# Mixing into z instead of the probabilities' buffer, and moving three weights' sums in a two-layer graph attention kernel

## The chip, the cores and the metric

The kernel runs on one core of a Trainium2 chip. Its time is the device time of one execution in microseconds (us); the median of three runs before the change is 2912.55 us (2912.05 to 2916.1). The engines are TensorE (PE, with its weight loads listed as PEld), VectorE (DVE), ScalarE (ACT) and GpSimd (POOL); SyncE (SP) issues all the DMA transfers.

## The reference

The input is `x`, 128 graphs of 64 nodes with 768 features, and a boolean adjacency for each graph. Two layers follow, each ended by a residual sum and a layer norm. All of it is float32.

```python
# layer 0: 12 heads of 64
h = einsum('bnd,ade->bane', x, W);  th = tanh(h)
attn = th @ w_src + swap(th @ w_dst)
attn = leaky_relu(attn, 0.2);  attn = where(~adj, -999, attn)
out = elu(softmax(attn) @ h + b)
gate = sigmoid(x @ H_w.T + H_b)
x = layernorm(x + gate * out + (1 - gate) * x)
# layer 1: 6 heads of 128
q, k, v = x @ Wq + bq, x @ Wk + bk, x @ Wv + bv
probs = softmax(q k^T / sqrt(128) + (0 or -9e15 by adj))
x = layernorm(x + (probs @ v) @ Wf + bf)
```

## The kernel before

**Tiles and stages.** Two graphs of 64 nodes make a tile of 128 rows, and two tiles make a pair; there are 64 tiles and 32 pairs. `phase_a` runs layer 0 on one pair after the other and also computes layer 1's values `v`, which it writes to DRAM together with the normalised rows and their transposes. `phase_b` then runs the rest of layer 1 on 16 groups of two pairs. Phase A takes the first 1511 us, phase B the other 1400.

**Products from fewer multiplications.** In phase A each product (h with `W`, the gate with `H_w`, v with `Wv`) is cut into two by two by two blocks and done in seven block products rather than eight (class `Product`). This needs sums of the activations' blocks (`token_sums`, four a pair, on POOL, L258 to L261) and sums of the weights' blocks, which are made once (`weight_sums`, L173). A product has seven steps `i = 0..6` of matmuls (L209); each is followed by an eviction from PSUM: a copy into a `snap` buffer or into the result on ACT (L418, L439, L458), or the sum of the bank and a `snap` on DVE (L441, L460). Step 4 adds onto the bank that the `snap` of step 2 reads, and step 6 onto the bank that DVE reads after step 4, so these matmuls wait for those reads. Phase B's products use another scheme of the same kind with 15 steps (class `Stream`, L875), 11 sums of activations (`group_sum`, L845) and 14 sums of 128x512 for each weight (`weight15_sum`, L167).

**What a tile passes through** (class `Tile0`): `tanh`; `dst_mul` and `src_mul` on POOL (L482, L490) with sums on DVE; a round trip through DRAM that spreads the `dst` part over the rows (`dst_out` L500, `dst_in` L508); `add` on ACT (twelve L532); `mask` and `top` on DVE (L539, L543); `exp` on ACT (twelve L548); `scale` on POOL (L558); `probs`, six transposes on PE (L569) and two copies on ACT into the buffer `pt` (L574); `aggregate`, the matmuls with `pt` as one operand (L587); `elu`, which adds the bias into `z` on DVE (L608) and takes the exponential of `z` on ACT (L616) into a tile `e`; `mix1` and `mix2`, four operations on DVE (L620, L621, L629, L630) that write `e`, and at last the row `xt`; `norm1` (L284, L293, L295 on DVE, then L296, L300, L301 on POOL) and `norm2` (L305 on ACT; in the last pair L639 on DVE); and the store `spill`.

The buffers named `pt`, `z`, `th` and `tmp` exist once each. The tile `e` takes the name `pt`, so it lies where the probabilities were; only the last pair puts it into `th` or `tmp`.

**The order.** It is written out by hand. `at(step, f)` notes a function for a step, and `run` calls all functions step by step; each engine executes its own instructions in this order. Pair `p` begins at step `O[p]`, which is 0, 14, 28 for the first three pairs and then 21 apart: `h` takes steps `o` to `o+6`, the gate `o+7` to `o+13`, and seven steps for the values of an earlier pair fill the rest. The pair's tile 1 has its times counted from `s = o`, tile 0 from `s = o+5` (in the last pair `o+3`): `probs` at `s+24`, `aggregate` at `s+25`, `elu`, `mix1` and `mix2` at `s+26` to `s+28`, the norm after that. So tile 1's `mix2` stands at `o+28` and tile 0's `probs` at `o+29`. After the last pair's gate come three earlier pairs' values, up to `o+34`; the last pair's own values stand at `o+45` to `o+51`, behind its norm, two transposes of its rows and its token sums. Phase B begins right behind them, on DVE with the sums L845.

**Weights.** Wv's four blocks are loaded at steps 10, 15, 20 and 25 (L177) and their twelve sums made on POOL at steps 30 to 52; the first values are due at step 56. Wq and Wk are loaded while the last pair runs; Wq's 14 sums stand on POOL from `o+21`, Wk's on DVE from `o+36`. Wf's sums follow on POOL in phase B.

Of the kernel before, what the change touches and what calls it, by code (L numbers as in the profile page):

```python
# [9 lines left out]
F32 = mybir.dt.float32  # L10
U8 = mybir.dt.uint8
AF = mybir.ActivationFunctionType
ALU = mybir.AluOpType
AX = mybir.AxisListType

P = 128
# [45 lines left out]
def kernel(  # L62
# [31 lines left out]
    nc = tc.nc  # L94
    NB, S, D = x.shape
# [7 lines left out]
    NP = NT // 2  # L103
# [40 lines left out]
    def weight_tile(tag):  # L144
        return wts.tile([P, 7, CH, HALF], F32, name=f"w{tag}", tag=f"w{tag}")
# [19 lines left out]
    def weight15_sum(wb, k, eng):  # L165
        to, a, b, sign = WEIGHT_SUMS[k]
        eng.tensor_tensor(wb[:, to], wb[:, a], wb[:, b], SIGN[sign])  # L167

    def weight_sums(part, eng, ks=range(4)):

        for k in ks:
            to, a, b = ((3, 6, 4), (4, 4, 0), (2, 6, 4), (5, 1, 2))[k]
            eng.tensor_tensor(part(to), part(a), part(b), ALU.subtract)  # L173

    def weight_plain(wb, src, blocks):
        for kh, oh in blocks:
                nc.sync.dma_start(  # L177
                    wb[:, SLOT[kh, oh]],
                    src[kh * HALF : (kh + 1) * HALF, oh * HALF : (oh + 1) * HALF].rearrange(
                        "(p c) o -> p c o", p=P  # L180
                    ),
                )
# [125 lines left out]
    def phase_a(ctx):  # L308
        k6 = ctx.enter_context(tc.tile_pool(name="k6", bufs=2))
        k3 = ctx.enter_context(tc.tile_pool(name="k3", bufs=1))  # L310
# [17 lines left out]
        def load_adj(p):  # L328
            t = small.tile([P, 2, S], U8, name="adj")
            nc.sync.dma_start(t, adj_p[p])  # L330
            st[p]["adj"] = t

        def load(p):
            st[p]["x"] = []
            for i in range(2):
                t = xb[:, (0, 1, 5, 6)[(2 * p + i) % 4]]
                nc.sync.dma_start(t, x_t[2 * p + i])
                st[p]["x"].append(t)
# [40 lines left out]
        w2 = weight_tile(2)  # L379
# [89 lines left out]
        class Tile0:  # L469
# [133 lines left out]
            def elu(self):  # L603

                self.z = k3.tile([P, D], F32, name="z")
                zv = self.z.rearrange("p (j h e) -> p j h e", h=2, e=E)
                for h2 in range(2):
                    nc.vector.tensor_tensor(  # L608
                        zv[:, :, h2, :],
                        self.pos[h2],  # L610
                        b_bc[:, None, :].to_broadcast([P, A // 2, E]),
                        ALU.add,
                    )

                self.e = k3.tile([P, D], F32, name=("th", "tmp")[self.i] if self.last else "pt")
                nc.scalar.activation(self.e, self.z, AF.Exp, bias=neg_one)  # L616

            def mix1(self):
                e, z = self.e, self.z
                nc.vector.scalar_tensor_tensor(e, e, 1.0, z, op0=ALU.min, op1=ALU.max)  # L620
                nc.vector.scalar_tensor_tensor(  # L621
                    e, e, 1.0, self.d["x"][self.i], op0=ALU.subtract, op1=ALU.subtract
                )

            def mix2(self):


                e, xt = self.e, self.d["x"][self.i]
                nc.vector.scalar_tensor_tensor(e, self.g, 1.0, e, op0=ALU.add, op1=ALU.mult)  # L629
                nc.vector.scalar_tensor_tensor(xt, xt, 4.0, e, op0=ALU.mult, op1=ALU.add)  # L630

            def norm1(self):
                self.stats = layernorm(small, self.d["x"][self.i], 4.0 * EPS, self.last)
# [17 lines left out]
        def at(step, *fs):  # L651
            events.setdefault(max(step, 0), []).extend(fs)
# [5 lines left out]
        for c in range(CH):  # L658
            at(0, lambda c=c: weight_sums(lambda s: w0_v[:, s, :, c, :], nc.vector))
            for k in range(4):  # L660
                at(
                    30 + 8 * c + 2 * k,
                    lambda c=c, k=k: weight_sums(lambda s: w2[:, s, c], nc.gpsimd, [k]),
                )
        for oc in range(NC):
            at(oc // 2 + 2, lambda oc=oc: hw_blocks(oc))

        for k, block in enumerate(((0, 0), (1, 0), (0, 1), (1, 1))):
            at(10 + 5 * k, lambda block=block: weight_plain(w2, Wv, [block]))

        at(9, lambda: nc.vector.tensor_scalar_add(b_bc, b_bc, 1.0))

# [3 lines left out]
        for p in range(NP):  # L676
            d, o = st[p], O[p]
            d["p"] = p
            if p:
                at(max(o - 20, 1), lambda p=p: load_adj(p))  # L680
                at(o + 8, lambda p=p: load(p))

            def xb_in(d, i):
                d.setdefault("xp", []).append(blocks(x_t[2 * d["p"] + i]))

            def xT(d, i):
                d.setdefault("T", []).append(turn(d["xp"][i]))

            if p:
                at(max(o - 20, 1), lambda d=d: xb_in(d, 0))  # L690
                at(max(o - 16, 1), lambda d=d: xb_in(d, 1))
                at(o - 6, lambda d=d: xT(d, 0))
                at(o - 5, lambda d=d: xT(d, 1))
                at(o - 4, lambda d=d: sums(d))
            else:
                at(0, lambda d=d: d.update(T=[transposed(t) for t in d["x"]]))
                at(0, lambda d=d: sums(d))
            at(o, lambda d=d: start_h(d))
            at(o + 7, lambda d=d: start_g(d))
            for i in range(7):  # L700
                at(o + i, lambda d=d, i=i: dense(d, "W", i))
                at(o + 7 + i, lambda d=d, i=i: dense(d, "G", i))
            for i, s in ((1, o), (0, o + (3 if p == NP - 1 else 5))):
                t = Tile0(p, i)
                at(s + 6 + (i == 0), t.tanh, t.cap)
                at(s + 7, t.dst_mul)
                at(s + 8, t.src_mul)
                at(s + 9, t.dst_sum, t.dst_out)
                at(s + 10, t.src_sum)
                at(s + 13, t.dst_in)  # L710
                at(s + 16, t.exchange)

                at(s + (15 if i else 17), lambda t=t: t.add(0))
                at(s + (16 if i else 17), lambda t=t: t.add(1))
                at(o + (14 if i else 16), t.gate_in)
                at(o + (17 if i else 18), t.gate)
                n = s - (i == 1)
                at(n + 18, t.mask, t.top)
                at(n + 19, lambda t=t: t.exp(0))
                at(n + 20, lambda t=t: t.exp(1))  # L720
                at(s + 21, lambda t=t: t.scale(0), lambda t=t: t.scale(1))
                at(s + 24, t.probs)
                at(s + 25, t.aggregate)
                at(s + 26, t.elu)
                at(s + 27, t.mix1)
                at(s + 28, t.mix2)
                at(s + 29, t.norm1)
                at(s + 30, t.norm2)
                at(s + 31, t.spill)

            def x1_in(d, i):
                d["xp", i] = blocks(x1_d[2 * d["p"] + i])

            def x1T(d, i, t):
                d["x1T", i] = t
                nc.sync.dma_start(xT_d[d["p"]][:, i], t)

            def x1_sums(d):
                d["T"] = [d["x1T", i] for i in range(2)]
                sums(d)  # L740

            if p < NP - 3:
                v = O[p + 3] + 14
                times = ((1, v - 19, v - 13), (0, v - 16, v - 10))
            elif p < NP - 1:

                v = O[-1] + (21 if p == NP - 3 else 28)
                times = ((1, v - 16, v - 7), (0, v - 15, v - 6)) if p == NP - 3 else (
                    (1, v - 12, v - 7), (0, v - 10, v - 6)
                )  # L750
            if p < NP - 1:
                for i, t0, t1 in times:
                    at(t0, lambda d=d, i=i: x1_in(d, i))
                    at(t1, lambda d=d, i=i: x1T(d, i, turn(d["xp", i])))
                at(times[1][2] + 1, lambda d=d: x1_sums(d))
            else:
                v = o + 45
                for i in range(2):
                    at(o + 43 - i, lambda d=d, i=i: x1T(d, i, transposed(d["x"][i])))
                at(o + 44, lambda d=d: x1_sums(d))  # L760
            at(v, lambda d=d: start_v(d))
            for i in range(7):
                at(v + i, lambda d=d, i=i: dense(d, "V", i))
# [5 lines left out]
        o = O[-1]  # L769
        early = []  # L770
# [7 lines left out]
            at(o + (7 + k if k < 4 else 8 + 2 * k), lambda k=k: load_early(0, Wq, k))  # L778
            at(o + 20 + 2 * k, lambda k=k: load_early(1, Wk, k))
        for k in range(len(WEIGHT_SUMS)):  # L780
            at(o + 21 + k // 2, lambda k=k: weight15_sum(early[0], k, nc.gpsimd))
            at(o + 36 + k, lambda k=k: weight15_sum(early[1], k, nc.vector))
        at(o + 30, lambda: load_T4(0))
        run(events, O[-1] + 80)
        return early
# [402 lines left out]
    with tc.manual_schedule():  # L1188
        with ExitStack() as c:
            early = phase_a(c)  # L1190
# [33 lines left out]
```

## Time and profile before

| stretch of the trace, us | length | PE busy | DVE busy | ACT busy | POOL busy |
|---|---|---|---|---|---|
| 0 to 60 | 60 | 47.18 | 28.07 | 18.22 | 19.83 |
| 60 to 100 | 40 | 37.00 | 30.17 | 29.37 | 25.96 |
| 100 to 140 | 40 | 32.28 | 32.05 | 25.44 | 35.07 |
| 140 to 190 | 50 | 42.31 | 39.99 | 30.34 | 30.36 |
| 240 to 1380 | 1140 | 1112.67 | 825.83 | 697.86 | 612.74 |
| 1430 to 1480 | 50 | 46.37 | 32.05 | 26.52 | 36.60 |
| 1480 to 1511 | 31 | 27.11 | 26.80 | 5.68 | 13.17 |
| 1540 to 2911 | 1371 | 1360.91 | 749.99 | 303.95 | 666.83 |

The profiled execution spans 2910.7 us at a mean granted PE clock of 0.996. The table gives, for stretches of the trace, the microseconds in which each engine was busy. A wait that costs something is one that leaves PE idle; idle time of the others costs nothing by itself.

How to read a line of the profile: `L574 ACT COPY pt<-pa` is line 574 of the kernel, on ACT, a copy from a PSUM tile `pa` into `pt`. In a list of waits, `PE pa L587 <- ACT pt L574: 35.5, 31, 3.0` says that PE's instruction of line 587 sat waiting for ACT's of line 574, 35.5 us in total, 31 times, 3.0 us the longest. A row of the timeline has the start, the duration (from the first to the end of the last, where several are merged), engine, line, operation, tiles, count, and in brackets how long the engine had been idle and for whom.

### The profile page before, as it was taken

Reading aid. Unit: us, or ns where it says so; the run is one execution under the profiler, and the core shown is the slowest. Engines: PE = TensorE matmul, PEld = TensorE weight load, DVE = VectorE, ACT = ScalarE, POOL = GpSimd, SP = SyncE. Lnnn points to the kernel's source line nnn. Section 1 sums busy time; section 2 is a strip of 40 time slices with the busy share of each in tenths; the row PEclk is TensorE's granted clock in tenths of the full one; section 3 lists DMA queues with packets and bytes.
Section 4 is the critical chain, followed back from the end, with each engine's and each line's share of the span. In section 5 each row is a group of like instructions: output and inputs, shape, how many; then the busy total and the mean of one; then the engine's idle time right before and its main releaser. Section 6 shows DMA issues by size and latency. Waiting matters only on the chain.

```text
span 2910.7 us, 50738 instructions
## 1 busy us (share of the span) xinstructions
PE 2831.1 (97%) x18108; PEld 2067.9 (71%) x18108; DVE 1852.5 (64%) x3716; ACT 1206.6 (41%) x3737; POOL 1510.3 (52%) x1633
## 2 busy tenths in 40 slices
PE   8889999999999999999999999999999999999998
PEld 5455555555555555555568888888888888888887
DVE  4886777767777777677765555555555555555556
ACT  4656566565665656656532212222211222211223
POOL 3855555555455554555553454455454455454455
PEclk9999999999999999999999999999999999999999
DMA  6435344353443534435461212122212222212222
GB/s 168 111 110 149 114 138 138 119 153 113 139 135 116 153 117 140 137 110 152 146 212 30 71 61 77 62 81 88 74 59 77 78 67 88 83 56 71 88 82 72
DMA packets 358683, 308.40 MB, mean 106 GB/s; under 512 B 226592, under 2 KB 304160, under 8 KB 358432
## 3 DMA queue, kind: packets, MB, share of 16 engines
q1 hardware_dynamic: 358432, 305.16, 34.4%
q8 instruction: 144, 2.36, 0.3%
q14 instruction: 107, 0.88, 0.1%
HBM read 191.41 MB, written 101.06 MB: 100 GB/s over the span
## 4 chain that ended last, share of the span: by engine, by line
PE 82%; DVE 11%; ACT 3%; issue 1%; POOL 1%; SPq 1%; DMA 1%; DVEq 0%; POOLq 0%; ACTq 0%
PE X L875 42%; PE X L209 33%; DVE pt L629 3%; PE pa L587 2%; PE pb L1015 2%; PE pb L940 2%; DVE pt L620 2%; DVE xb L630 1%; DVE pt L621 1%; ACT pt L616 1%; DVE z L608 1%; PE pb L995 1%; ACT s L548 1%; PE pa L569 1%; ACT pt L574 0%
## 5 line engine op out<-in xcount | busy, mean ns | idle before, releaser
L209 PE MATMUL X<-w,S 128*128 128x384 f32 x2304 | 801.7, 493 | 19.6 <-ACT snap L418 10.3
L875 PE MATMUL X<-S,w 128*128 128x256 f32 x2816 | 664.7, 382 | 1.1 <-DVE S L845 0.8
L209 PEld LDWEIGHTS X<-w,S 128*128 128x128 f32 x2304 | 431.7, 191 | 310.4 <-ACT snap L418 12.5
L209 PE MATMUL X<-w,T 128*128 128x384 f32 x1728 | 599.5, 490 | 5.6 <-ACT snap L418 3.5
L875 PEld LDWEIGHTS X<-S,w 128*128 128x128 f32 x2816 | 525.0, 190 | 73.6 <-DVE S L845 1.5
L209 PEld LDWEIGHTS X<-w,T 128*128 128x128 f32 x1728 | 327.8, 192 | 230.3 <-issue 7.8
L857 POOL TENSOR_TENSOR Sc<-cT 128x256 f32<-128x256 f32 x224 | 161.2, 726 | 405.5 <-PE X L875 399.3
L875 PE MATMUL X<-w,Sc 128*128 128x256 f32 x1408 | 322.5, 381 | 0.8 <-DVE xs L918 0.8
L918 DVE TENSOR_TENSOR xs<-xs,X 128x256 f32<-128x256 f32 x512 | 210.4, 419 | 169.0 <-PE X L875 160.1
L875 PEld LDWEIGHTS X<-w,Sc 128*128 128x128 f32 x1408 | 265.5, 190 | 38.3 <-DVE xs L918 1.6
L548 ACT ACTIVATE s<-s,nmx 128x64 f32<-128x64 f32 x768 | 256.2, 335 | 43.1 <-DVE nmx L543 43.1
L901 DVE TENSOR_TENSOR k<-k,X 128x256 f32<-128x256 f32 x320 | 133.5, 421 | 216.2 <-PE X L875 165.8
L901 DVE TENSOR_TENSOR q<-q,X 128x256 f32<-128x256 f32 x320 | 133.2, 420 | 182.1 <-PE X L875 146.4
L875 PE MATMUL X<-xb,w 128*128 128x256 f32 x960 | 236.6, 379 | 0.0
L305 ACT ACTIVATE xs<-xs,shift,rstd 128x768 f32<-128x768 f32 x62 | 63.5, 1025 | 417.3 <-POOL shift L301 396.8
L896 ACT ACTIVATE k<-X,bk_c 128x256 f32<-128x256 f32 x192 | 91.0, 474 | 305.1 <-PE X L875 305.1
L896 ACT ACTIVATE q<-X,bq_c 128x256 f32<-128x256 f32 x192 | 90.8, 473 | 279.5 <-PE X L875 279.5
L418 ACT COPY snap<-X 128x384 f32<-128x384 f32 x288 | 136.5, 474 | 168.6 <-PE X L209 163.8
L875 PEld LDWEIGHTS X<-xb,w 128*128 128x128 f32 x960 | 181.2, 190 | 24.0
L532 ACT ACTIVATE s<-s,src 128x64 f32<-128x64 f32 x768 | 193.3, 336 | 8.8 <-DMA s<-dst_d 8.6
L482 POOL TENSOR_TENSOR tmp<-th,wd_bc 128x768 f32<-128x768 f32 x64 | 120.9, 1889 | 145.1 <-ACT th L478 145.1
L296 POOL TENSOR_TENSOR rstd<-rstd,neg_half 128x1 f32<-128x1 f32 x126 | 69.1, 548 | 235.7 <-DVE rstd L295 235.4
(129 smaller groups left out, 4085.6 us busy)
## 6 DMA issues: line engine op xcount, KB each, us to landing
xb<-in_x_dram SPq DMA_DIRECT2D x64, 384.0 KB
s<-dst_d SPq DMA_DIRECT2D x128, 192.0 KB
x_d<-xb SPq DMA_DIRECT2D x64, 384.0 KB
xT_d<-T SPq DMA_DIRECT2D x64, 384.0 KB
v_d<-v SPq DMA_DIRECT2D x128, 192.0 KB
xb<-xT_d SPq DMA_DIRECT2D x32, 768.0 KB
xb<-v_d SPq DMA_DIRECT2D x256, 96.0 KB
xs<-x_d SPq DMA_DIRECT2D x64, 384.0 KB
```

The costliest lines, as they stand in the source:

```text
L209: nc.tensor.matmul(o, self.lhsT(i, c), rhs, start=first and c == 0, stop=last and c == CH - 1, skip_group_check=True,)
L296: nc.gpsimd.tensor_tensor(rstd, rstd, neg_half, ALU.pow)
L418: nc.scalar.copy(t, ps)
L482: nc.gpsimd.tensor_tensor(self.tmp, self.th, wd_bc, ALU.mult)
L532: nc.scalar.activation(self.s[:, a], self.s[:, a], AF.Prelu, bias=self.src[:, a : a + 1], alpha=LEAKY_ALPHA,)
L548: nc.scalar.activation(self.s[:, a], self.s[:, a], AF.Exp, bias=self.nmx[:, a : a + 1], accum_out=self.sm[:, a : a + 1],)
L629: nc.vector.scalar_tensor_tensor(e, self.g, 1.0, e, op0=ALU.add, op1=ALU.mult)
L857: nc.gpsimd.tensor_tensor(t, pair_part(d, q, r0), pair_part(d, q, r1), op)
L875: nc.tensor.matmul(ps, self.lhsT(r, slot, c), self.rhs(r, slot, c), start=start and c == 0, stop=stop and c == 1, skip_group_check=True,)
L896: nc.scalar.activation(o[:, b], ps, AF.Identity, bias=bias[:, hd : hd + 1], scale=1.0 if positive else -1.0)
L901: nc.vector.tensor_tensor(o[:, b], o[:, b], ps, ALU.add if positive else ALU.subtract)
L918: nc.vector.tensor_tensor(o, o, ps, ALU.add if positive else ALU.subtract)
```

## The change

There are three parts.

- `mix1` and `mix2` write their intermediate results to `z` rather than to `e`, so that the buffer `pt`, in which `e` lies, has its last reader in the first operation of `mix1` rather than in the last of `mix2`. The last pair's `e` goes to `pt` too, and the last pair's tile 0 starts at `o+4` instead of `o+3`.
- The third weight, Wv, is loaded at steps 2 to 5 and its sums are made at steps 13 to 24 on POOL.
- Wq's sums go to DVE from step `o+44`, Wk's to POOL from step `o+45`, both beside the last pair's values.

It is meant to free the probabilities' buffer earlier, and to take weight sums out of stretches in which the engines also have a pair's softmax to do.

```diff
-                self.e = k3.tile([P, D], F32, name=("th", "tmp")[self.i] if self.last else "pt")
+                self.e = k3.tile([P, D], F32, name="pt")
                 nc.scalar.activation(self.e, self.z, AF.Exp, bias=neg_one)
 
             def mix1(self):
                 e, z = self.e, self.z
-                nc.vector.scalar_tensor_tensor(e, e, 1.0, z, op0=ALU.min, op1=ALU.max)
+                nc.vector.scalar_tensor_tensor(z, e, 1.0, z, op0=ALU.min, op1=ALU.max)
                 nc.vector.scalar_tensor_tensor(
-                    e, e, 1.0, self.d["x"][self.i], op0=ALU.subtract, op1=ALU.subtract
+                    z, z, 1.0, self.d["x"][self.i], op0=ALU.subtract, op1=ALU.subtract
                 )
 
             def mix2(self):
-                e, xt = self.e, self.d["x"][self.i]
-                nc.vector.scalar_tensor_tensor(e, self.g, 1.0, e, op0=ALU.add, op1=ALU.mult)
-                nc.vector.scalar_tensor_tensor(xt, xt, 4.0, e, op0=ALU.mult, op1=ALU.add)
+                z, xt = self.z, self.d["x"][self.i]
+                nc.vector.scalar_tensor_tensor(z, self.g, 1.0, z, op0=ALU.add, op1=ALU.mult)
+                nc.vector.scalar_tensor_tensor(xt, xt, 4.0, z, op0=ALU.mult, op1=ALU.add)
...
                 at(
-                    30 + 8 * c + 2 * k,
+                    13 + 4 * c + k,
                     lambda c=c, k=k: weight_sums(lambda s: w2[:, s, c], nc.gpsimd, [k]),
                 )
...
         for k, block in enumerate(((0, 0), (1, 0), (0, 1), (1, 1))):
-            at(10 + 5 * k, lambda block=block: weight_plain(w2, Wv, [block]))
+            at(2 + k, lambda block=block: weight_plain(w2, Wv, [block]))
...
-            for i, s in ((1, o), (0, o + (3 if p == NP - 1 else 5))):
+            for i, s in ((1, o), (0, o + (4 if p == NP - 1 else 5))):
...
-            at(o + 21 + k // 2, lambda k=k: weight15_sum(early[0], k, nc.gpsimd))
-            at(o + 36 + k, lambda k=k: weight15_sum(early[1], k, nc.vector))
+            at(o + 44 + k // 2, lambda k=k: weight15_sum(early[0], k, nc.vector))
+            at(o + 45 + k // 2, lambda k=k: weight15_sum(early[1], k, nc.gpsimd))
```

## The prediction

> **What bounds the kernel now.** I read the page's busy shares first, then its chain of waits, then PE's own waits, then the timeline of one pair.
>
> ```profile
> PE 2831.1 (97%) x18108; PEld 2067.9 (71%) x18108; DVE 1852.5 (64%) x3716; ACT 1206.6 (41%) x3737; POOL 1510.3 (52%) x1633
> PE 82%; DVE 11%; ACT 3%; issue 1%; POOL 1%; SPq 1%; DMA 1%; DVEq 0%; POOLq 0%; ACTq 0%
> ...
> PE pa L587 <- ACT pt L574: 35.5, 31, 3.0
> ...
> ACT pt L574 <- DVE xb L630: 86.4, 31, 5.2
> ```
>
> TensorE (PE) is 97% busy, so a change that leaves its matmuls alone can win at most its idle time: 2910.7 - 2831.1 = 79.6 us, plus what a slowed PE clock costs. The chain is PE's, but 11% of it runs through VectorE (DVE). The two waits (total us, times, longest) say where: the copy of the probabilities into `pt` (L574) waits 31 times for the last multiply-add of `mix2` (L630), and the aggregation (L587) waits for that copy, 35.5 us of idle PE. That is the largest wait PE has; the next, for `snap` (L418), is 13.9 us. By place: PE idles 12.8 us before 60 us, 18.2 us from 60 to 190, and from 205 to 1429 us only this wait appears, once a pair: 28 gaps, 45.3 us apart, 1.08 us each (one of 1.36). Then some 8 us up to the start of layer 1 at 1511, and only about 3 us in layer 1.
>
> One such pair, columns start and duration in us, engine, line, operation, and idle before in brackets:
>
> ```profile
> 742.28 1.58 DVE L620 SCALAR_TENSOR_TENSOR pt<-pt,z 128x768 f32<-128x768 f32 x1
> 743.89 0.96 DVE L621 SCALAR_TENSOR_TENSOR pt<-pt,xb 128x768 f32<-128x768 f32 x1
> ...
> 744.90 2.57 DVE L629 SCALAR_TENSOR_TENSOR pt<-gp,pt 128x768 f32<-128x768 f32 x1
> ...
> 745.25 0.82 PE L569 MATMUL pa<-ident,s 128*128 128x128 f32 x6
> ...
> 745.90 2.10 PE L209 MATMUL X<-w,T 128*128 128x384 f32 x6
> 747.51 0.96 DVE L630 SCALAR_TENSOR_TENSOR xb<-xb,pt 128x768 f32<-128x768 f32 x1
> ...
> 748.55 0.86 ACT L574 COPY pt<-pa 128x384 f32<-128x384 f32 x2 [2.63 <-DVE xb L630]
> 749.08 0.27 PE L587 MATMUL pa<-xb,pt 64*64 64x64 f32 x1 [1.08 <-ACT pt L574]
> ...
> 752.28 0.48 ACT L418 COPY snap<-X 128x384 f32<-128x384 f32 x1
> ```
>
> The reader is to see: `pt` is free only at 748.5, though the transposes (L569) that fill it were done at 745.9. Their product step hides 2 us of that; the rest stops PE.
>
> **What the Trainium skill says.** (1) In "SBUF — State Buffer", section "Who interferes with whom": a VectorE instruction with two SBUF inputs contends with a GpSimd (POOL) instruction that reads SBUF, by a lock held for the whole instruction. The trace agrees in kind: L621, L629 and L630 take 0.96 us alone, 1.9 in the last pair beside POOL's weight sums (L167), up to 2.57 here beside L482; a POOL sum of 128x512 takes 1.29 alone (14 in 18.06 us) and about 2.0 then. (2) In "TensorE: Matmul & The Clock Gate", "What's actually happening": idle PE falls to half its clock and must be busy again for a while. The trace agrees: after gaps of 2.2 to 3.0 us the next six matmuls take 3.7 to 3.9 us, not 2.1; after 1.08 us they don't. (3) The same page's table: ScalarE (ACT) is a strict FIFO. The trace agrees: every `snap` behind a waiting L574 or L305 comes late.
>
> **The change part by part.**
>
> *Mix in z.* No instruction is added or removed; L620, L621, L629 write `z`, and `pt` is free after L620, at 743.9. L574 then runs at about 745.95, right behind a `snap`, and ends near 746.9; the aggregation can start when its product step ends, 747.9. The other tile of each pair shows an unhindered passage: its transposes start at 733.86 and the next product step after aggregation at 737.40, 3.54 us. Here it is 745.25 to 750.04, 4.79. So 1.25 us a pair may go.
> A wait follows close behind. ACT's next are L305 (norm) and the `snap` at 752.28, which PE needs two steps later. L305 waits for DVE's run L620 to L295 and POOL's rstd; that run starts from an eviction ahead of the aggregation (741.58), so it doesn't move. The snap ends at 752.76. PE, with 1.25 us gone, wants that bank at 748.79 (745.25 + 3.54) plus two steps of 1.93, that is 752.65. It waits about 0.2 us. Gain per pair 1.05; times 28, plus 0.28 for the odd one: **29.7 us**. `z` is held until L630 instead, but its next writer L608 follows L630 on DVE itself: nothing.
>
> *Wv early.* Four loads of 0.59 MB go from behind each pair's traffic (issued 46.95 to 75.34) to about 27 us, behind the second pair's x. At the 176 GB/s of the first 60 us, 2.36 MB takes 13 us: there at 43, before POOL reaches the first sum (about 51, behind L482). The 12 sums move from 90-153 us to about 51-75 us, where POOL idles 7.5 + 4.8 us and more. Queued behind them are scale (L558), L490, L597: at most 1 to 2 us late, in a stretch where ACT and DVE wait for DMA anyway. What goes away: contention and delay at 90-153, among it POOL's two stalls of PE at 120 us (1.02 + 0.96, and 1.7 of slow clock). The gap at 87.5 us (3.0, and 1.6 slow) is L574's, but behind it the snap waits for L305 at 90.5, so most of it comes back. Seven of the 12 sums took 1.7 us, not 1.0, and the DVE operations beside them lost about as much, some 5 us. I take **5 us** gained, bounds -3 (scale late) and 12 (half of the stalls and slow clock).
>
> *Last pair.* Wq's 14 sums leave POOL at 1460-1487:
>
> ```profile
> 1473.70 13.08 POOL L167 TENSOR_TENSOR w<-w 128x512 f32<-128x512 f32 x8
> 1481.06 1.91 DVE L630 SCALAR_TENSOR_TENSOR xb<-xb,tmp 128x768 f32<-128x768 f32 x1
> 1487.11 3.65 PE L209 MATMUL X<-w,S 128*128 128x384 f32 x6 [2.94 <-ACT snap L418]
> 1494.93 9.55 DVE L167 TENSOR_TENSOR w<-w 128x512 f32<-128x512 f32 x10
> ```
>
> Four mix operations fall from 1.9 to 0.96 (3.8 us), POOL's rstd is 1.6 us earlier, and the gap of 2.94 with its slow clock (1.8) should close. One step more for the second tile (o+4) costs 1.93 on its chain, but lets tile 1's `dst_in` go ahead of tile 0's `dst_out`, and a `snap` go ahead of twelve L532: the gaps at 1449.87 (2.21, and 1.8 slow) and 1462.64 (1.14) should shrink. `e` in `pt` again instead of `th`, `tmp` costs nothing, as L620 frees it a step before. All gaps would be 10; the second tile's chain keeps some. **6 us** gained, bounds 2 and 9.
>
> *Start of layer 1.* Here it costs. Before, POOL idles from 1501.9 to 1520.9 and DVE ends Wk's sums beside the last values. Now both sum at once. Ten DVE sums in 9.55 us beside POOL's four token sums: 5.65 us contended, 3.9 alone at 0.67, hence 1.36 contended; beside 512-wide POOL sums between 1.34 and 1.96 (0.67 + 1.29, strict turns); I take 1.66. From the start of V (call it 0, before at 1496.6): four DVE sums to 2.4, an eviction at 4.5, six to 14.2, then the eviction that V's last product waits for (due 11.6; PE stalls 3), two, an eviction, two, to 21.9; then the first layer-1 sum (L845), to 23.6. Before, layer 1 began at 14.7. POOL's Wk sums last until about 28, needed only after 15 more steps. Some L845 still contend: 2 us. With turns of 1.34 the first L845 ends at 20.3 and the loss is 7; with 1.66, 11. I take **9 us** lost, bounds 2 and 14.
>
> Sum: -29.7 - 5 - 6 + 9 = -31.7; 2912.55 - 31.7 = 2880.9, say **2881**.
>
> **Rivals.** (a) *The ends cost little*: ACT, DVE and POOL slack at the entry absorbs the sums, and the head gives 10: -29.7 - 10 - 6 + 2 = 2869. For it: DVE is idle a quarter of 1511-1524. Against: contended sums are seen at twice their time. (b) *The wait moves*: the snap behind L305 eats half of the steady gain, 14.7: 2896. For it: today the snap is ready 1.15 us before PE asks (750.04 + 2 x 1.93 = 753.90 against 752.76), less than the 1.25 that goes. Against: the run ahead of it doesn't depend on the aggregation, so it shouldn't come later. (c) *Slower*: DVE's run is the true period, so only 3 of the 29.7 come; early sums hold up scale (+5), nothing at the tail, 14 at the entry: 2929. Against: DVE is busy 32.8 of 45.3 us and waits for PE several times in each pair. (d) *No change*: half the steady gain, 14 lost at the entry, nothing at the other places: about 2912.
>
> **Numbers.** Forecast 59%, (a) 18%, (b) 15%, (c) 4%, (d) 4%. The range reaches past (a) and to (b): 2866 to 2897. Faster 0.92, same 0.04, slower 0.04.
>
> **What would show it.** L587's wait for L574 gone from PE's waits, pair period 44.2 to 44.3 instead of 45.3, perhaps a small new `snap` gap two steps after. No POOL L173 after 80 us, and fewer gaps at 120. In the last pair mix operations near 0.96 and V starting 6 us sooner relative to the pair before. Then DVE L167 at 1.3 to 1.7 us each, and a PE gap `X L875 <- DVE S L845` of several us. I am wrong if the period stays above 44.8, if that gap is under 2 us, or if PE waits for the early sums between 50 and 90 us.

## The result, and the profile after

The changed kernel takes 2882.85 us (median of four runs, 2881.09 to 2884.16), against 2914.01 us for the kernel before on the same chip: a ratio of 0.9893, 95% interval [0.9875, 0.991]. The profiled executions span 2880.6 and 2910.7 us, 30.2 us apart before rounding. The forecast was 2881.

After the change every line number from L616 on is one higher, and the old L616 is L615. The page's busy shares and its chain of waits:

```profile
PE 2825.0 (98%) x18108; PEld 2061.9 (72%) x18108; DVE 1877.8 (65%) x3716; ACT 1201.5 (42%) x3737; POOL 1535.4 (53%) x1633
PE 86%; DVE 6%; POOL 3%; DMA 2%; issue 1%; ACT 1%; SPq 1%; DVEq 0%; POOLq 0%; ACTq 0%
```

DVE's part of the chain fell from 11% to 6% and PE's rose from 82% to 86%, yet DVE is busy 25 us longer in all, and POOL too. Something was taken out of PE's path, and instructions elsewhere became longer. PE's waits (total us, times, longest) say what:

```profile
PE X L209 <- ACT snap L418: 10.9, 6, 3.6
...
PE X L876 <- DVE S L846: 5.9, 4, 4.1
PE X L209 <- DVE v L460: 3.5, 3, 2.6
...
PE pa L587 <- DMA v_d<-v: 3.1, 1, 3.1
PE pa L412 <- DVE xb L639: 2.2, 1, 2.2
```

The 35.5 us of L587 behind L574 are gone from this list; one wait of L587 is left, of 3.1 us, which the list puts down to a transfer (see e7). The waits for `S` (layer 1's first token sums) and for `v`, 0.8 and 0.4 us before, have grown, and the one for L639 is new. The copy's own group, with its idle time and what ended it in the last column, changed in the same way:

```profile
L574 ACT COPY pt<-pa 128x384 f32<-128x384 f32 x128 | 55.4, 486 | 3.8 <-PE pa L569 3.8
```

**By stage.** To compare runs I cut each trace at the same six instructions, read from its timeline: the transposes of the fourth pair's tile 0 (end of the head); tile 0's aggregation in the pair before the last (28 such aggregations later); the first matmul of the last pair's values, V; the first matmul of layer 1; the start of its second product, k. All in us:

| kernel | head | steady | last pair | V to layer 1 | first product, q | rest | span |
|---|---|---|---|---|---|---|---|
| before | 201.5 | 1227.5 | 67.6 | 14.7 | 13.1 | 1386.4 | 2910.7 |
| after | 196.5 | 1193.1 | 63.6 | 22.3 | 17.6 | 1387.5 | 2880.6 |
| e1_mix_only | 201.9 | 1192.9 | 68.5 | 14.7 | 13.1 | 1386.9 | 2877.9 |
| e2_old_layer1_sums | 195.3 | 1193.5 | 71.3 | 16.3 | 13.1 | 1387.2 | 2876.7 |
| e3_old_Wv | 202.2 | 1193.5 | 66.1 | 23.3 | 15.9 | 1391.5 | 2892.6 |
| e4_sums_apart | 193.1 | 1192.8 | 65.2 | 16.3 | 13.1 | 1386.6 | 2867.1 |
| e5_Wk_writes_only | 194.1 | 1193.3 | 65.8 | 14.7 | 13.1 | 1391.2 | 2872.0 |
| e6_norm_behind_snap | 191.6 | 1198.3 | 66.5 | 23.3 | 15.9 | 1390.1 | 2885.7 |
| e7_o3 | 196.5 | 1192.4 | 65.0 | 23.1 | 16.6 | 1390.6 | 2884.2 |
| e8_all | 190.3 | 1197.5 | 65.3 | 16.9 | 13.1 | 1387.2 | 2870.2 |
| e9_norm_late_in_head | 190.3 | 1192.8 | 63.7 | 16.3 | 13.1 | 1387.9 | 2864.1 |
| e10_load_late | 196.7 | 1192.4 | 63.6 | 15.7 | 13.1 | 1386.7 | 2868.1 |

Each row is one profiled execution. The rows after, e2, e4, e5, e7 and e10 have the same head, and it took 193.1 to 196.7: a head is known to some 2 us only. The last pair is no better known: after, e3 and e5 have the same instructions there (e6 too, but for the norm of the pair before it), and it took 63.6, 66.1, 65.8 and 66.5. The granted PE clock in that stretch was 1.00 of full speed in the trace of after, 0.97, 0.97 and 0.94 in the three others, and 0.95 before the change. The steady column, with the same instructions in most rows, repeats within 1.2 us.

One steady pair after the change, the same stretch as the prediction showed of before (start, duration, engine, line, operation, idle before in brackets):

```profile
722.70 1.58 DVE L620 SCALAR_TENSOR_TENSOR z<-pt,z 128x768 f32<-128x768 f32 x1
...
725.33 2.57 DVE L629 SCALAR_TENSOR_TENSOR z<-gp,z 128x768 f32<-128x768 f32 x1
725.67 0.82 PE L569 MATMUL pa<-ident,s 128*128 128x128 f32 x6
...
726.24 0.87 ACT L574 COPY pt<-pa 128x384 f32<-128x384 f32 x2
726.32 2.10 PE L209 MATMUL X<-w,T 128*128 128x384 f32 x6
727.94 0.96 DVE L630 SCALAR_TENSOR_TENSOR xb<-xb,z 128x768 f32<-128x768 f32 x1
728.35 0.27 PE L587 MATMUL pa<-xb,pt 64*64 64x64 f32 x1
```

L574 no longer stands behind L630: it runs at 726.24, while L629 is still writing `z`, and the aggregation starts at 728.35, right behind its product step. And ACT, a little later:

```profile
731.58 1.03 ACT L305 ACTIVATE xb<-xb,shift,rstd 128x768 f32<-128x768 f32 x1 [4.47 <-POOL shift L301]
732.52 0.46 ACT L418 COPY snap<-X 128x384 f32<-128x384 f32 x1
```

This `snap` is the one I expected PE to wait for. It ends at 732.98. PE's product step after the aggregation starts at 729.21, and two steps of 1.93 later it wants the bank, at 733.07. It doesn't wait. From 240 to 1380 us PE now has no wait in the trace's list, and from 300 to 1380 it is busy 1079.80 of 1080 us. Of the 27 pair periods in the steady stretch, 25 are 44.06 us; two are 0.35 and 0.39 us longer, behind another `snap` (see e6).

The start of layer 1. Before the change PE had no wait ahead of V's last product, and a short one at layer 1's first:

```profile
1508.31 2.10 PE L209 MATMUL X<-w,S 128*128 128x384 f32 x6
1511.25 1.13 PE L875 MATMUL X<-S,w 128*128 128x256 f32 x4 [0.84 <-DVE S L845]
```

After it, first DVE, then POOL and PE:

```profile
1457.93 9.16 DVE L167 TENSOR_TENSOR w<-w 128x512 f32<-128x512 f32 x6
1467.01 0.55 DVE L460 TENSOR_TENSOR v<-X,snap 128x384 f32<-128x384 f32 x1
...
1473.70 5.09 DVE L846 TENSOR_TENSOR S<-xb 128x512 f32<-128x512 f32 x3
```

```profile
1456.90 23.02 POOL L167 TENSOR_TENSOR w<-w 128x512 f32<-128x512 f32 x14
```

```profile
1467.70 3.74 PE L209 MATMUL X<-w,S 128*128 128x384 f32 x6 [2.60 <-DVE v L460]
1475.50 3.40 PE L876 MATMUL X<-S,w 128*128 128x256 f32 x8 [4.06 <-DVE S L846]
```

Six of Wq's sums took DVE 9.16 us (the first 0.80, the five others 1.63 to 1.75 each) and three token sums 5.09, or 1.7 each, while POOL spent 1.64 us on each of Wk's. The eviction L460 that V's last product needs stood in that queue, and PE lost 2.60 and 4.06 us, each with a slowed clock after it: six matmuls in 3.74 us (2.10 in a steady pair), eight in 3.40 (1.99 in e5).

### The profile page after: what moved, and what is told of

It reads as the page before. It is cut to its first block, busy times and chain, and to the rows that moved or that the text cites. A ratio compares the mean times of both kernels' runs of the same rounds, so it can differ in the third digit from the quotient of the medians.

```text
span 2880.6 us, 50750 instructions
## 1 busy us (share of the span) xinstructions
PE 2825.0 (98%) x18108; PEld 2061.9 (72%) x18108; DVE 1877.8 (65%) x3716; ACT 1201.5 (42%) x3737; POOL 1535.4 (53%) x1633
## 4 chain that ended last, share of the span: by engine, by line
PE 86%; DVE 6%; POOL 3%; DMA 2%; issue 1%; ACT 1%; SPq 1%; DVEq 0%; POOLq 0%; ACTq 0%
PE X L876 42%; PE X L209 37%; PE pb L1016 2%; PE pb L941 2%; PE pa L587 2%; PE pa L569 1%; DVE z L629 1%; PE pb L996 1%; DVE z L620 1%; DVE S L846 0%; DVE w L173 0%; POOL th L490 0%; POOL w L173 0%; DVE st L284 0%; DVE xb L630 0%
## 5 line engine op out<-in xcount | busy, mean ns | idle before, releaser
L209 PE MATMUL X<-w,S 128*128 128x384 f32 x2304 | 800.8, 493 | 18.2 <-ACT snap L418 7.4
L548 ACT ACTIVATE s<-s,nmx 128x64 f32<-128x64 f32 x768 | 256.2, 335 | 76.8 <-DVE nmx L543 76.8
L305 ACT ACTIVATE xs<-xs,shift,rstd 128x768 f32<-128x768 f32 x62 | 63.5, 1025 | 419.0 <-POOL shift L301 412.4
L482 POOL TENSOR_TENSOR tmp<-th,wd_bc 128x768 f32<-128x768 f32 x64 | 141.4, 2210 | 126.8 <-ACT th L478 126.8
L532 ACT ACTIVATE s<-s,src 128x64 f32<-128x64 f32 x768 | 193.3, 335 | 15.0 <-DMA s<-dst_d 14.4
```

The source lines that it names most:

```text
L209: nc.tensor.matmul(o, self.lhsT(i, c), rhs, start=first and c == 0, stop=last and c == CH - 1, skip_group_check=True,)
L305: nc.scalar.activation(r, r, AF.Identity, bias=shift, scale=rstd)
L482: nc.gpsimd.tensor_tensor(self.tmp, self.th, wd_bc, ALU.mult)
L532: nc.scalar.activation(self.s[:, a], self.s[:, a], AF.Prelu, bias=self.src[:, a : a + 1], alpha=LEAKY_ALPHA,)
L548: nc.scalar.activation(self.s[:, a], self.s[:, a], AF.Exp, bias=self.nmx[:, a : a + 1], accum_out=self.sm[:, a : a + 1],)
```

## The experiments

**e1_mix_only: the first part alone.** Wv's loads and sums, the layer-1 sums and the last pair's start are those of before.

```diff
-                    13 + 4 * c + k,
+                    30 + 8 * c + 2 * k,
-            at(2 + k, lambda block=block: weight_plain(w2, Wv, [block]))
+            at(10 + 5 * k, lambda block=block: weight_plain(w2, Wv, [block]))
-            for i, s in ((1, o), (0, o + (4 if p == NP - 1 else 5))):
+            for i, s in ((1, o), (0, o + (3 if p == NP - 1 else 5))):
-            at(o + 44 + k // 2, lambda k=k: weight15_sum(early[0], k, nc.vector))
-            at(o + 45 + k // 2, lambda k=k: weight15_sum(early[1], k, nc.gpsimd))
+            at(o + 21 + k // 2, lambda k=k: weight15_sum(early[0], k, nc.gpsimd))
+            at(o + 36 + k, lambda k=k: weight15_sum(early[1], k, nc.vector))
```

> The kernel after with only the first part of the change: mix in z and the last pair's e in pt; Wv's loads and sums, Wq's and Wk's sums and the last pair's o+3 as before. My theory: the steady pairs give their 1.25 us each (34.4 us between 205 and 1429 us of the trace of before), the head about 1, the last pair nothing, so about 2878, with L1 starting some 14.7 us after the last values start. Rival, that the moved sums carry a good part of the gain: 2890 or more.

Measured: 2879.76 us, ratio 0.9881 [0.9866, 0.9895]. The whole steady gain is there (1192.9), and nothing else: the head stays at 201.9 and the last pair at 68.5. So the first part alone does about as well as all three together: its interval overlaps that of the changed kernel. In the head the wait for `pt`, 3.00 us at 87.5 before, came back one link further on, 7 us later:

```profile
94.63 4.21 PE L209 MATMUL X<-w,S 128*128 128x384 f32 x6 [3.98 <-ACT snap L418]
```

That is the "most of it comes back" of the prediction: a `snap` queued on ACT behind L305.

**e3_old_Wv: the second part undone.** From the changed kernel, Wv's loads and sums are put back (the first four lines of the diff above).

> The kernel after with Wv's loads at steps 10 to 25 and its sums at steps 30 to 52, as before. My theory: the first 200 us lose the 4 to 5 us that they had won, nothing else changes: 2887. Rival, that the head's gain came from pt too: 2883, the same.

Measured: 2890.09 us, 0.9921 [0.9906, 0.9936]. The head goes back to 202.2. With e1 this settles the head: the three rows with late Wv take 201.5 to 202.2, the six with early Wv and the same norm 193.1 to 196.7. Early Wv gives some 6 us there, and the mix gives none. The time is 3 us above its forecast, because the rest is 4.0 us longer than in the changed kernel. The trace shows a wait of 2.27 us there for an eviction of k on DVE, against 1.06 in the changed kernel. e5, e6 and e7, whose rest is long too, have one of 1.95 to 2.26. Why it comes in some kernels and not in others wasn't settled.

**e2_old_layer1_sums: the third part undone** (the last four lines of the same diff, from the changed kernel; the last pair still starts tile 0 at `o+4`).

> The kernel after with Wq's and Wk's sums where they stood before (Wq on POOL from o+21, Wk on DVE from o+36). My theory: the new place cost 13.3 us between the start of the last values and the end and gave about 4 in the last pair, so undoing it gains about 9: 2873, layer 1 starting 14.7 us after the last values. Rival: the last pair's mix beside POOL's sums now holds pt, as e is in pt again, and the PE gaps of the last pair return in full: 2880 to 2886, no gain.

Measured: 2877.2 us, 0.9874 [0.9859, 0.9889]. The forecast was 2873, the rival's 2880 to 2886: it lies between. The entry is back at 16.3 + 13.1, 10.5 us less than in the changed kernel, but the last pair takes 71.3, 5 to 8 us more than the 63.6 to 66.5 of the kernels with the moved sums. A wait of PE in that stretch that the changed kernel doesn't have:

```profile
1437.49 0.55 PE L569 MATMUL pa<-ident,s 128*128 128x128 f32 x3 [2.78 <-POOL s L558]
```

The transposes wait for `scale` on POOL, because Wq's sums stand ahead of it there and one of them waited 3.6 us for Wq's load. So, in a kernel that has the other two parts, the third takes 5 to 8 us out of the last pair and pays about 10.5 us for it at the entry. The intervals of e2 and of the changed kernel overlap a little, so that it is a net loss is likely, not certain.

**e5_Wk_writes_only: is it contention?** POOL's 14 sums for Wk are replaced by fills of the same tiles, which write and don't read. Wk's sums are left out.

```diff
-            at(o + 45 + k // 2, lambda k=k: weight15_sum(early[1], k, nc.gpsimd))
+            at(o + 45 + k // 2, lambda k=k: nc.gpsimd.memset(early[1][:, WEIGHT_SUMS[k][0]], 0.0))
```

> The kernel after with Wk's 14 sums on POOL replaced by 14 fills of the same blocks with zero, which read nothing from SBUF (Wk's sums are left out, so layer 1's keys are not the reference's). My theory, that the loss at the start of layer 1 is DVE's two-input sums held up by POOL's reads: L167 and L846 on DVE fall from 1.5 and 1.7 us to about 0.67, the PE gap before layer 1 from 4.1 to about 1, the first q stream from 17.6 to 13, total about 2871. Rival, that it is the order on DVE, 14 sums between the evictions of the last values: the sums' durations hardly matter, the gap stays above 3 us, 2880.

Measured: 2875.76 us, 0.987 [0.9854, 0.9887]. The groups of the two DVE sums, busy us and mean ns of one, in the changed kernel:

```profile
L167 DVE TENSOR_TENSOR w<-w 128x512 f32<-128x512 f32 x14 | 18.2, 1326 | 0.2
L846 DVE TENSOR_TENSOR S<-xb 128x512 f32<-128x512 f32 x9 | 10.9, 1238 | 0.0
```

and with POOL filling:

```profile
L167 DVE TENSOR_TENSOR w<-w 128x512 f32<-128x512 f32 x14 | 9.9, 734 | 0.2
L783 POOL MEMSET w<- 128x512 f32 x14 | 6.7, 524 | 0.1
L846 DVE TENSOR_TENSOR S<-xb 128x512 f32<-128x512 f32 x9 | 5.9, 685 | 0.1
```

DVE does exactly the same sums in the same order in 9.9 rather than 18.2 us, and the entry takes 14.7 + 13.1 as before the change. The six sums that run beside the fills take 0.68 to 0.69 us each, no more than alone. Since fourteen DVE sums still stand beside the last values, it isn't their place that costs, but what POOL reads at that time. The time is 5 us above the forecast, 3.7 of it in the long rest named under e3. POOL is also done sooner here, 6.7 us against 23, but PE needs nothing of Wk's before k, so that alone couldn't shorten the entry.

**e7_o3: where the last pair's tile 0 starts** (`o+3` again, all else changed).

```diff
-            for i, s in ((1, o), (0, o + (4 if p == NP - 1 else 5))):
+            for i, s in ((1, o), (0, o + (3 if p == NP - 1 else 5))):
```

> The kernel after with the last pair's tile 0 at o+3, as before. My theory: with POOL free of Wq's sums one step costs about what it is, the tile's chain ends 0 to 2 us earlier or PE's gaps before 1450 return; within 2 us of the kernel after: 2881 to 2885. Rival, that o+4 is what won the last pair's 4 us (it lets dst_in and a snap go ahead): 2887.

Measured: 2885.43 us, 0.9901 [0.9887, 0.9916]. Its interval overlaps that of the changed kernel, and its last pair, 65.0, lies among the 63.6 to 66.5 that `o+4` gave, so neither step is shown to be better. One set of waits is exchanged for another. With `o+3` a `snap` is late (3.74 us at 1411.18), and the waits of 3.13 and 2.23 us for L574 and L639 are gone. With `o+4` tile 1's copy L574 stands on ACT behind tile 0's exponentials, as ACT's and PE's rows of the changed kernel show:

```profile
1425.92 0.35 ACT L548 ACTIVATE s<-s,nmx 128x64 f32<-128x64 f32 x1 [2.50 <-DVE nmx L543]
...
1428.28 0.85 ACT L574 COPY pt<-pa 128x384 f32<-128x384 f32 x2
```

```profile
1428.81 0.27 PE L587 MATMUL pa<-hp,pt 64*64 64x64 f32 x1 [3.13 <-DMA v_d<-v]
```

The wait list names a transfer for this gap, but the aggregation starts as soon as the first of the two copies into `pt` is done, at 1428.75, and its weight load waits for L574 by name.

**e4_sums_apart: Wq's and Wk's sums mostly where the other engine doesn't sum.** Wq is loaded sooner; eleven of its sums go to POOL, at steps at which POOL had been idle, three to DVE; Wk's sums go back to DVE.

```diff
-            at(o + (7 + k if k < 4 else 8 + 2 * k), lambda k=k: load_early(0, Wq, k))
+            at(o + 7 + k, lambda k=k: load_early(0, Wq, k))
-            at(o + 44 + k // 2, lambda k=k: weight15_sum(early[0], k, nc.vector))
-            at(o + 45 + k // 2, lambda k=k: weight15_sum(early[1], k, nc.gpsimd))
+            t = (18, 18, 21, 21, 21, 24, 24, 26, 26, 29, 29, 36, 36, 36)[k]
+            eng = nc.gpsimd if k < 11 else nc.vector
+            at(o + t, lambda k=k, eng=eng: weight15_sum(early[0], k, eng))
+        for k in range(len(WEIGHT_SUMS)):
+            at(o + 36 + k, lambda k=k: weight15_sum(early[1], k, nc.vector))
```

> The kernel after with Wq's loads at o+7 to o+12, eleven of Wq's sums on POOL in the gaps of the last pair where DVE has no two-input work from SBUF (two at o+18, three at o+21, two each at o+24, o+26, o+29), the other three and all of Wk's on DVE from o+36, so that POOL and DVE never sum at once for long. My theory: it keeps the last pair's gain (last values start about 66 us after tile 0's transposes of the pair before) and loses none of the 12 us at the start of layer 1: 2871. Rival, that sums in the last pair delay it wherever they stand (as in e2): last values 4 to 7 us later, 2876.

Measured: 2871.29 us, 0.9855 [0.9839, 0.9872]. This is as forecast: both the short last pair (65.2) and the short entry (16.3 + 13.1) are there.

**e6_norm_behind_snap: take the late `snap` out of the head.** From the changed kernel: the norm L305 on ACT and the store behind it one step later, except in the last pair; with it the load of `x` must come later.

```diff
-                at(o + 8, lambda p=p: load(p))
+                at(o + 9, lambda p=p: load(p))
-                at(s + 30, t.norm2)
-                at(s + 31, t.spill)
+                at(s + (30 if t.last else 31), t.norm2)
+                at(s + (31 if t.last else 32), t.spill)
```

> The kernel after with every pair's norm2 (L305 on ACT) and spill one step later, but for the last pair, and load(p) at o+9 for it. My theory: what stops PE in the first 200 us now is the snap that stands behind L305, so the gaps at 92.9, 129.8 and 169.6 us (2.6, 3.6 and 3.1 us, two with slow clock behind them) go or halve, 6 to 10 us: 2875. In the steady pairs nothing changes. Rival, that DVE's run of mix and norm is what is late there: the next wait takes over, under 2 us gained: 2882.

Measured: 2886.23 us, 0.9904 [0.9889, 0.9919]: no gain. The head is shorter (191.6), but the steady stretch, in which nothing was to change, takes 5.2 us more and eats it. Of its 27 pair periods 12 are 44.06 us as in the changed kernel and 15 are 0.06 to 0.79 us longer. The loss is always at the same place: PE's second product step after tile 1's aggregation waits for a `snap`, and that `snap` stands on ACT behind six of tile 0's exponentials (L548). These wait for L543 on DVE, which needs the result of tile 0's twelve L532, and L532 waits for the transfer at the end of the round trip of `dst`. That last wait, first in the changed kernel, then in e6:

```profile
ACT s L532 <- DMA s<-dst_d: 14.4, 21, 2.5
ACT s L532 <- DMA s<-dst_d: 33.5, 29, 2.4
```

Counted from the L569 of tile 0 in the pair before, the pairs that lose nothing start these L532 at 30.60 us or sooner, in both kernels, and every pair that loses more than 0.01 us starts them at 30.64 or later (the two longer pairs of the changed kernel at 30.94 and 30.98). In e6 a store of the pair before is issued 23.1 to 23.7 us after that L569, rather than 18.5 to 20.2, so it stands closer ahead of the transfer; that its traffic is what delays the transfer is likely, but not tested.

**e8_all** put e4 and e6 together, and loaded the first adjacency of layer 1 sooner:

> e4 and e6 together, and in layer 1 the first mask's load ahead of Wf's (its DVE operation stays where it is), so that it no longer holds the k evictions on DVE behind it. My theory: the gains add up, 12 at the start of layer 1, 6 to 10 in the head, 1 to 3 from the mask: 2862. Rivals: as those of e4 and e6, 2872 or more.

Measured: 2868.68 us, 0.9848 [0.9833, 0.9862]. It missed its forecast in the same way: the steady stretch is 1197.5, and the sooner load shows no gain in the rest (1387.2 against e4's 1386.6).

**e9_norm_late_in_head and e10_load_late: which edit of e6 costs, and where.** Both start from e4. e9 delays norm, store and load for the first pairs alone; e10 delays only the load, from the fifth pair on.

```diff
 e9
-                at(o + 8, lambda p=p: load(p))
+                at(o + (9 if p < 4 else 8), lambda p=p: load(p))
-                at(s + 30, t.norm2)
-                at(s + 31, t.spill)
+                at(s + (31 if p < 4 else 30), t.norm2)
+                at(s + (32 if p < 4 else 31), t.spill)
 e10
-                at(o + 8, lambda p=p: load(p))
+                at(o + (9 if p >= 4 else 8), lambda p=p: load(p))
```

> As e4_sums_apart, but norm2 and spill stand one step later for the first four pairs alone, and the loads of the second to fourth pair at o+9. Theory: the two gains add where each was seen. The head falls from 193.1 to some 190 to 191.5 (e6 and e8 gave 191.6 and 190.3), the steady pairs stay at 1192.8 to 1193.5, since every later pair has its norm where e4 has it; time 2868 to 2869 (e4: 2871.3). Rival: the steady loss of e6 comes out of how the head hands over, and not from the late norm in each pair; then the steady stretch is 1197 to 1198 here too and the time is 2873.

> As e4_sums_apart, but the load of x stands at o+9 rather than o+8 from the fifth pair on; norm2 and spill as in e4. It parts the two edits of e6 in the steady pairs. If the late load costs e6's 5 us there, the steady stretch is 1197 to 1198 and the time 2876. If the late norm does (my guess, as PE's only listed waits there are for snap, behind L305 on ACT), the steady stretch stays at 1192.8 to 1193.5 and the time at 2871.

Measured: e9 2866.11 us, 0.9842 [0.9828, 0.9855], steady 1192.8, head 190.3; e10 2871.78 us, 0.9856 [0.9843, 0.987], steady 1192.4. So the late load costs nothing in the steady pairs, and the late norm with its store costs the 5 us there; in the head alone it wins some 5 us. The guess that came with e10, a `snap` behind L305, was wrong on the path: the late `snap` stands behind L548 and, through it, L532, as shown above. e9 has the lowest median of these kernels, and its interval lies wholly under that of the changed kernel, though not under those of e4 and e8.

## Why the prediction was right, and where its terms were off

The sum held because it was right on which part carries it, and by luck in the rest: the steady pairs gave 4.7 us more than forecast, the last pair, the start of layer 1 and the rest together 6.2 us less, and the two nearly cancelled.

| term | forecast, us | measured, us | settled by |
|---|---|---|---|
| steady pairs | -29.7 | -34.4 | e1: the mix alone gives it |
| head | -5 | -5.0 | e1 and e3: all of it is Wv's |
| last pair | -6 | -4.0 (-1.1 to -1.8 with e3's, e5's and e6's traces) | not settled: see below |
| start of layer 1 | +9 | +12.1 (7.6 to layer 1, 4.5 in q) | e2, e4, e5 |
| rest | 0 | +1.1 | |
| sum | -31.7 | -30.2 | |

**Steady pairs: mechanism right, term too small.** The pair's period, 45.3 us before, is 44.06: below the forecast 44.2 to 44.3, and the full 1.25 us that the comparison with the other tile's passage had given. What failed is "It waits about 0.2 us". That sum set the `snap`'s end, 7.51 us after the start of L569 (752.76 - 745.25), as if the chain of L305 had fixed it. Now it ends after 7.31 (732.98 - 725.67). L305 itself did stay where I had put it: it starts 5.90 us after L569 in the trace of before and 5.91 now. But before, the `snap` began 0.10 us after L305's end (752.28 against 752.18), and now it begins 0.09 ahead of it (732.52 against 732.61). Before, it had been held by something else, most likely its own product step on PE, which began at 750.04 and takes 2.10; that part moved with PE. Rival (b), half of the gain eaten by that `snap`, is out. But the margin is only 0.1 us (732.98 against 733.07). Nor is it the only one: the `snap` behind L548 (see e6) has little to spare as well, and there two pairs of the changed kernel and 15 of e6 do pay.

**Head: size right.** POOL made its twelve sums by 75.1 us, among L482, L490 and L597, and no PE wait over 0.6 us appears between 50 and 80 us, so early sums held up nothing that mattered. Of the two stalls at 120 us one of 0.58 is left, but `scale` now holds PE up a pair sooner, at 81 to 83 us (0.32 and 0.96). The return of the `pt` gap at 87.5 as a `snap` was foreseen and is seen in e1. Not foreseen: another such `snap` wait, 1.90 at 132.97 before, grew to 3.63 at 129.82. The heads with the later norm (e6, e8, e9) take 190.7 on average, the six others with early Wv 195.4: these waits, with the clock behind them, are worth some 5 us.

**Last pair: the old waits went, but new ones came; too large by a third or more.** All eight mix operations there take 0.95 or 0.96 us, as forecast, V starts 4 rather than 6 us sooner relative to the pair before, and the three `snap` gaps of before are gone. Two waits that the prediction didn't have took their place: 3.13 for L574 behind the exponentials and 2.23 for L639 ahead of the last transposes; e7, with `o+3`, has neither. The step at fault is "All gaps would be 10; the second tile's chain keeps some": it left 4 us for that chain, and the two new waits alone are 5.4. PE's listed gaps in this stretch fell from 6.9 to 6.1 us only. Most of the 4.0 is the clock: before, two gaps had a half-clock stretch behind them, and in this one trace none had, although gaps as long remained. In e3, e5 and e6 some did, and there V starts only 1.1 to 1.8 us sooner than before.

**Start of layer 1: mechanism shown, term too small.** The forecast had the first L845 done 23.6 us after V's start and PE stalled 3 us at V's last product. Layer 1 began at 22.3, and the stall was 2.60. The 1.66 taken for a contended sum was right: seven of Wq's ten took 1.63 to 1.75 us; the other three, only partly beside POOL's sums, took 0.80 and 1.28 twice, which makes up the difference. What was too cheap is "Some L845 still contend: 2 us": q alone took 4.5 us longer. The first group's eleven token sums took DVE 15.1 us rather than 7.3 as in e5. POOL was at Wk's sums until 1479.9, and from 1481.87 on at Wf's, whose 14 sums I had left out: before the change these began at 1520.94, when Wf's load had come, just behind the last token sum (1519.73); now they fell on the rest of them. PE paid with four waits of 0.21 to 0.84 us within q, besides the slow clock at its start. e5 shows the cause: without POOL's reads in Wk's place both numbers are back at 14.7 and 13.1. It also bears out what the prediction drew from the Trainium skill ("SBUF — State Buffer", section "Who interferes with whom"): the page says that a two-input DVE instruction contends with a POOL instruction that reads SBUF, not with one that only writes it; DVE's sums beside POOL's fills took 0.68 to 0.69 us, beside POOL's sums 1.63 to 1.75.

**The rivals.** (a), slack at the entry absorbs the sums: out, by the 12.1 us. (b) out, as said. (c), DVE's run as the true period: out, by a PE that waits for nothing in the steady pairs. (d) needed half of (b).

## What to carry to other kernels

Where one buffer name serves two uses, look at who reads it last: writing intermediate results into an operand that dies anyway can let the next use begin several operations sooner, at no instruction's cost. Then follow the chain two links on and measure the margin of the next wait. Before you place sums on DVE and POOL "beside each other", ask what both read: work that looks parallel in a schedule cost 12.1 us here at the start of layer 1, and the same sums, placed mostly where POOL had been idle, cost 1.7 there. And before you put a few us down to an edit, look at the same stretch in kernels that share its instructions, and at the granted clock there.

## What the runs showed of the hardware

- DVE sums of two 128x512 operands took 0.69 us alone, 0.68 to 0.69 beside POOL fills of 128x512 (0.52 us each), and 1.63 to 1.75 when they ran wholly beside POOL's own two-operand sums. (The group means above, 0.73 and 1.33, mix these.) POOL's sums went from 1.28 (25 in 31.5 us in e4) to 1.64 us. Beside each other DVE thus lost a factor of about 2.5, POOL 1.3. They went one for one: in the changed kernel POOL's sums start at 1459.81, 1461.60, 1463.16 and 1464.83, and DVE's 0.5 to 0.6 us after each, at 1460.43, 1462.11, 1463.67 and 1465.45. One of each took about 1.67 us, less than the 0.69 + 1.28 = 1.97 of strict turns.
- The length of a gap alone doesn't tell whether PE's clock slows after it; its place does. The prediction had said that after 2.2 to 3.0 us the next six matmuls take 3.7 to 3.9 us. A gap of 2.40 us for `hp` gave 3.85 in the trace of before (139.51) and 2.20, no loss, in e3 (140.20); in the changed kernel 2.64 gave 3.71 (92.93) and 3.12 gave 2.20 (169.61). The granted clock in the traces sorts these out. In each trace it changes on a grid of equal steps of 3.41 us, and falls to half for one step, now and then for two and once for four; one step at half clock costs 1.7 us. Over the twelve traces, leaving out the first 20 and the last 8 us, each of the 56 full-clock steps in which PE idled for 1.97 us or more was followed by a step at half clock, none of the 99 with 1.0 to 1.72 us was, and 3 of the 14 in between were. The gap of 2.64 us lies with 2.29 in one step (89.17 to 92.58); the gap of 3.12 is cut by a grid line at 167.67 into 1.18 and 1.94. The section of the Trainium skill that the prediction named for this ("TensorE: Matmul & The Clock Gate", "What's actually happening") gives one idle window of about 3.4 us for the fall; here about 2 of 3.41 us was enough. Where the grid lies against the kernel's start differs from trace to trace, and this is part of why the head and the last pair are known to 2 or 3 us only.
